# Layer 1's experts in two lots of sequences, with the last sequence's end and the first lot's last sums in gaps of the blocks

## The chip, the cores and the metric

The kernel runs on one core of one Trainium2 chip. The core has five instruction queues that run side by side: TensorE (PE, with its weight loads shown apart as PEld), VectorE (DVE), ScalarE (ACT), GpSimd (POOL) and SyncE (SP). Each runs its own instructions in order, and they wait for one another by semaphores. Transfers between the chip's large memory and the on-chip buffers are issued from SP, ACT and POOL. The metric is the device time of one execution in microseconds (us); the median over several runs is compared.

## The reference

Eight sequences of 512 tokens, 256 wide, in float32, pass through two layers. Each layer is attention, then a mixture of experts, each with the input added and a layer norm after it:

```python
x = _layernorm(x + _L0_attn_ref(x, ...))
x = _layernorm(x + _L0_ffn_ref(x, ...))
x = _layernorm(x + _L1_attn_ref(x, ...))
x = _layernorm(x + _L1_ffn_ref(x, ...))
```

The change concerns the last line. Of twelve experts in layer 1, eight are small networks and four return the token itself. Each token takes its two best:

```python
logits = jnp.einsum('btd,ed->bte', x, gate_w) + expert_bias
topk_logits, topk_idx = jax.lax.top_k(logits, TOP_K)
topk_w = jax.nn.softmax(topk_logits, axis=-1)
...
h = jax.nn.silu(jnp.einsum('btd,efd->btef', x, w1))      # 256 -> 512
y = jnp.einsum('btef,edf->bted', h, w2)                  # 512 -> 256
out = jnp.einsum('bte,bted->btd', w_ffn, y) + w_zero[..., None] * x
```

The kernel computes an expert only for the tokens that chose it.

## The kernel before

Layer 0 and layer 1's attention run in "waves": sixteen waves for each sequence. One wave computes a quarter of the scores of four heads (`scores`), lets ACT make the sigmoids, and multiplies the wave before with the values (`gathered`). The order of all this is written out by hand: `beside1(b, w)` lists for each wave of sequence `b` which small steps of the neighbouring sequences stand beside it. For a sequence `a` those are, in this order: `by_token` and `by_feature` (transposes of the attention's output), `projected` (output projection, router logits and the sums for the norm), `normed3`, `logits`, `chosen` (the two best experts), `counted`, `ranked` (which row of the expert's list a token gets), `sent`, and, two sequences later, `scatter` (L1113), in which POOL writes each token's row, with its gates and its token number, to its place in a table `xbuf1` in the large memory.

Within `with tc.manual_schedule()` the instructions of each engine stand in the order in which the program writes them. Outside it a scheduler orders them.

The last sequence has no later waves to stand beside. So after `waves1(B - 1)` its steps run alone (L1522 to L1528): the last `scatter` of the sequence before, `by_token` to `sent`, its own eight scatters, and `planned` (L1134), which makes from the counts of all eight sequences the table of blocks.

A block is 256 rows of one expert's list. `plan` holds for block `j` its first row and its expert, `mine` a mask of the expert. The program always runs 26 blocks (`NTB0`); two run-time branches (L1636) add more if the counts ask for them. A block `j` has these parts:

- `load(j)` on SP: two register loads from `plan`, one transfer of the block's rows (`xt`), one for each of the expert's two weight matrices. It is called two blocks ahead.
- `turn`: four transposes on PE, a copy on ACT, and on DVE the block's gates `g` and its target rows `to`.
- `inner`: sixteen matmuls, the sigmoid on ACT, the product `h` on DVE.
- `outer`: sixteen matmuls, two scalings on DVE (`yt`), and two scatters on POOL into `ybuf1`, a table with two rows for each token.

In iteration `j` of `work` (L1613) PE's order is `turn(j + 1)`, `inner(j)`, `outer(j - 1)`.

After the blocks and the branches, for each of the eight sequences (L1640): two reads of `ybuf1` on SP, an addition on POOL (L1648) and one on DVE (L1649), the norm's statistics on DVE, a square root on ACT, scale and shift on ACT (L1661), and the output's transfer on ACT's queue (L1665).

Of the kernel before, what the change touches and what calls it, by code (L numbers as in the profile page):

```python
# [9 lines left out]
FP = mybir.dt.float32  # L10
I32 = mybir.dt.int32
# [18 lines left out]
NTB = 2 * NT // TB + E1 - 1  # L30
NTB0, NTB1 = 26, 32
EARLY = 5
NS1 = E1 * NT
# [10 lines left out]
def tile_two_layers(  # L44
# [91 lines left out]
    def row(pool, src, n, name):  # L136
# [5 lines left out]
    slot1 = const.tile([P, NC, E1], FP, name="slot1")  # L142
    nc.gpsimd.iota(
        slot1, pattern=[[0, NC], [NT, E1]], base=-NS1, channel_multiplier=0,
        allow_small_or_imprecise_dtypes=True,
    )

    tok = const.tile([P, B, NC], FP, name="tok")
    nc.gpsimd.iota(
        tok, pattern=[[S, B], [P, NC]], base=0, channel_multiplier=1,  # L150
        allow_small_or_imprecise_dtypes=True,
    )

    full = const.tile([P, E1, NT // TB], FP, name="full")
    nc.gpsimd.iota(
        full, pattern=[[0, E1], [TB, NT // TB]], base=0, channel_multiplier=0,
        allow_small_or_imprecise_dtypes=True,
    )
    block = const.tile([P, NTB], FP, name="block")
    nc.gpsimd.iota(  # L160
        block, pattern=[[1, NTB]], base=0, channel_multiplier=0,
# [12 lines left out]


    xbuf1 = dram.tile([NS1 + TB, XR], FP, name="xbuf1")
    ybuf1 = dram.tile([2 * NT, D], FP, name="ybuf1")
# [174 lines left out]
    def layer0():  # L352
# [64 lines left out]

        def fill(b, part):

            if b == 0:  # L420
                for e in range(2 * part, min(2 * part + 2, E0)):
                    nc.sync.dma_start(
                        out=xbuf[e * CAP : (e + 1) * CAP, :].rearrange("(p c) d -> p c d", p=P),
                        in_=zeros,
                    )
                if part == 3:
                    nc.sync.dma_start(out=ybuf[NSLOT : NSLOT + 1, :], in_=blank[0:1, :D])
                    nc.sync.dma_start(
                        out=xbuf1[NS1 : NS1 + TB, :].rearrange("(c p) d -> p c d", p=P), in_=blanks
                    )  # L430
            for i in range(4 * part, 4 * part + 4):
                at = (b * 16 + i) * 256
                nc.sync.dma_start(
                    out=xbuf1[at : at + 256, :].rearrange("(c p) d -> p c d", p=P), in_=blanks
                )

            if part % 2 == 0:
                at = (b * 2 + part // 2) * 512
                nc.sync.dma_start(
                    out=ybuf1[at : at + 512, :].rearrange("(p c) d -> p c d", p=P), in_=zeros  # L440
                )
# [323 lines left out]
    def layer1(turns):  # L765
# [292 lines left out]
        def counted(b):  # L1058
# [6 lines left out]
            nc.gpsimd.tensor_scalar(q["second"], hot[1][:, :, :E1], float(NT), None, ALU.mult)  # L1065
# [5 lines left out]
        def ranked(b):  # L1071
# [11 lines left out]
            nc.vector.tensor_tensor(q["slot"], pp, slot1, ALU.add)  # L1083
            nc.vector.tensor_copy(counts1[:, 0, :], counts1[:, NC, :])

        def sent(b):
# [10 lines left out]
            nc.vector.tensor_scalar(idx, sf, float(NS1), None, ALU.add)  # L1097
            for k in range(2):
# [9 lines left out]
                tok[:, b].unsqueeze(2).to_broadcast([P, NC, E1]), ALU.add,  # L1108
# [6 lines left out]
        def scatter(b, c):  # L1115
            q = st[b]
            for k in range(2):
                i = nc.gpsimd.indirect_dma_start(  # L1118
                    out=xbuf1[:, :],
# [3 lines left out]
                    bounds_check=NS1 - 1,  # L1123
                    oob_is_err=False,
                )
                apart("xbuf1", i, b == c == k == 0)
# [7 lines left out]
        def planned():  # L1134

            tp = bank()[:, :E1]
            nc.tensor.matmul(out=tp, lhsT=ones, rhs=counts1[:, 0, :], start=True, stop=True)
            more = planp.tile([P, E1, NT // TB], FP, name="more")
            nc.vector.tensor_tensor(more, tp.unsqueeze(2).to_broadcast([P, E1, NT // TB]), full, ALU.is_gt)
            held = planp.tile([P, E1], FP, name="held")  # L1140
            nc.vector.tensor_reduce(held, more, axis=AX.X, op=ALU.add)
            upto = planp.tile([P, E1], FP, name="upto")
            nc.vector.tensor_tensor_scan(upto, ones[:, :E1], held, 0.0, ALU.mult, ALU.add)
            nc.vector.tensor_copy(total, upto[:, E1 - 1 : E1])
            past = planp.tile([P, NTB, E1], FP, name="past")
            nc.vector.tensor_tensor(
                past, upto.unsqueeze(1).to_broadcast([P, NTB, E1]),
                block.unsqueeze(2).to_broadcast([P, NTB, E1]), ALU.is_le,
            )
            which = planp.tile([P, NTB], FP, name="which")  # L1150
            nc.vector.tensor_reduce(which, past, axis=AX.X, op=ALU.add)
            nc.vector.tensor_tensor(past, past, held.unsqueeze(1).to_broadcast([P, NTB, E1]), ALU.mult)
            start = planp.tile([P, NTB], FP, name="start")
            nc.vector.tensor_reduce(start, past, axis=AX.X, op=ALU.add)
            nc.vector.tensor_tensor(start, block, start, ALU.subtract)
            nc.vector.tensor_scalar(start, start, float(TB), None, ALU.mult)
            nc.vector.scalar_tensor_tensor(start, which, float(NT), start, ALU.mult, ALU.add)
            nc.vector.tensor_scalar(plan[:, 0, :], start, float(NS1), None, ALU.min)

            nc.vector.tensor_scalar(which, which, float(E1 - 1), None, ALU.min)  # L1160
            nc.vector.tensor_copy(plan[:, 1, :], which)
            nc.vector.tensor_tensor(
                mine, which.unsqueeze(2).to_broadcast([P, NTB, E1]),
                iota_e[:, 0:1, :E1].to_broadcast([P, NTB, E1]), ALU.is_equal,
            )

# [234 lines left out]
    def beside1(b, w):  # L1401
# [46 lines left out]
        return [[s for s in steps if 0 <= s[1] < B] for steps in plan[w]]  # L1448
# [50 lines left out]
    plan = planp.tile([P, 2, NTB], I32, name="plan")  # L1499
    mine = planp.tile([P, NTB, E1], FP, name="mine")  # L1500
    total = planp.tile([P, 1], I32, name="total")
# [15 lines left out]
    psum(ctx, 2, 2, 2)  # L1517
    with tc.manual_schedule():
# [4 lines left out]
        run([(t.scatter, b - 1, c) for c in range(NC)])  # L1523
        run([(t.by_token, b, c) for c in range(NC)])
        run([(t.by_feature, b, kc) for kc in range(KC)])
        run([(t.projected, b, c) for c in range(NC)])
        run([(fn, b) for fn in (t.normed3, t.logits, t.chosen, t.counted, t.ranked, t.sent)])
        run([(t.scatter, b, c) for c in range(NC)])  # L1528
        t.planned()
    work.close()  # L1530


    with ExitStack() as ph:
        moew = ph.enter_context(tc.tile_pool(name="moew1", bufs=2, side="right"))
        hp = ph.enter_context(tc.tile_pool(name="h1", bufs=3))
        sp = ph.enter_context(tc.tile_pool(name="s1", bufs=4))
        lp = ph.enter_context(tc.tile_pool(name="l1", bufs=3))

        def load(j):
            r = nc.sync.value_load(plan[0:1, 0, j : j + 1], min_val=0, max_val=NS1)  # L1540
            e = nc.sync.value_load(plan[0:1, 1, j : j + 1], min_val=0, max_val=E1 - 1)
            xt = sp.tile([P, TB // P, XR], FP, tag="xt", name="xt")
            nc.sync.dma_start(
                out=xt, in_=xbuf1[bass.ds(r, TB), :].rearrange("(c p) d -> p c d", p=P)
            )
            w = moew.tile([P, 2, KC * F1], FP, tag=("wi", "wo")[j % 2], name="w_e")
            wi = w[:, 0, :].rearrange("p (k f) -> p k f", f=F1)
            nc.sync.dma_start(
                out=wi, in_=w1[bass.ds(e, 1), :, :].rearrange("o (k p) f -> p (o k) f", p=P)
            )  # L1550
            wo = w[:, 1, :].rearrange("p (f d) -> p f d", d=D)
            nc.sync.dma_start(
                out=wo, in_=w2[bass.ds(e, 1), :, :].rearrange("o (f p) d -> p (o f) d", p=P)
            )
            return xt, wi, wo

        def turn(j, xt):

            ps = bank().rearrange("p (k t) -> p k t", t=TB)
            for kc in range(KC):  # L1560
                for c in range(TB // P):
                    nc.tensor.transpose(
                        ps[:, kc, c * P : (c + 1) * P], xt[:, c, kc * P : (kc + 1) * P], ident
                    )
            xtT = hp.tile([P, KC, TB], FP, tag="xtT", name="xtT")
            nc.scalar.copy(xtT, ps)
            gx = sp.tile([P, TB // P, 2, E1], FP, tag="gx", name="gx")
            nc.vector.tensor_tensor(
                gx, xt[:, :, D:XR].rearrange("p c (u e) -> p c u e", e=E1),
                mine[:, j : j + 1, :].unsqueeze(1).to_broadcast([P, TB // P, 2, E1]), ALU.mult,  # L1570
            )
            g = sp.tile([P, TB // P, 2], FP, tag="g", name="g")
            nc.vector.tensor_reduce(g, gx, axis=AX.X, op=ALU.add)
            to = sp.tile([P, TB // P], I32, tag="to", name="to")
            nc.vector.tensor_copy(to, g[:, :, 1])
            return xtT, g, to
# [185 lines left out]
```

## Time and profile before

| | us |
|---|---|
| median of 3 runs | 1662.85 |
| lowest, highest | 1657.31, 1667.59 |
| the profiled execution | 1652.81 |
| its span in the profile | 1651.0 |

| engine | busy us in the span | share |
|---|---|---|
| PE | 1445.3 | 88% |
| DVE | 891.3 | 54% |
| ACT | 677.9 | 41% |
| POOL | 469.1 | 28% |

Layer 0 takes up the span to about 869 us, layer 1's attention the stretch to about 1360, the blocks the stretch from 1400 to 1592, the last sums the rest. Several views are used below. The page divides the span in forty slices. A table of stretches gives, for windows chosen by the reader, each engine's busy time, the TensorE clock that was granted (1.00 is full speed) and the mean share of time in which the 16 DMA engines were busy. The timeline lists groups of instructions by their start, with the idle time of the engine ahead of them and what ended it in brackets. The chain of waits follows the work that ended last back from the end. A busy engine can be one that does more than it must, and idle time is a loss only where the next work had to wait for it.

### The profile page before, as it was taken

To read this page: it belongs to the slowest core of one execution; us is meant where nothing else is said; L and a number is where in the kernel's file an instruction comes from. 1 tells how busy PE (TensorE), PEld (TensorE's weight loads), DVE (VectorE), ACT (ScalarE), POOL (GpSimd) and SP (SyncE) were. 2 spreads that over 40 slices of the span, in tenths; PEclk is the share of its full clock that TensorE was granted. 3 is DMA by queue.
4 is the path that set the end of the run, shared out by engine and by line. 5 is a ranking of instruction groups with operands and counts; after the bars stand their busy time and mean duration, and the time that the engine had idled before them with its cause. 6 is when DMAs were issued, how large, how long until landed. Compare 5 with 4: busy or idle time off the path is not lost. (4 is left out here: it accounts for less than half of the span.)

```text
span 1651.0 us, 24593 instructions
## 1 busy us (share of the span) xinstructions
PE 1445.3 (88%) x8556; PEld 772.2 (47%) x8556; DVE 891.3 (54%) x3367; ACT 677.9 (41%) x1007; POOL 469.1 (28%) x596
## 2 busy tenths in 40 slices
PE   6999889898898789999989999999999993999950
PEld 3444444444444356566534333333333432888840
DVE  3666667666667512220356576677677644333327
ACT  2545445444444320101335666666566660222214
POOL 2221233233232300000251234354453333222233
PEclk8999999999998989999978999999999995999985
DMA  7869920000000102422010000120120003666637
GB/s 221 240 205 362 354 80 12 15 9 20 4 21 1 29 0 79 151 77 89 29 36 8 21 26 25 23 42 26 25 41 18 10 19 114 213 218 216 205 106 238
DMA packets 141385, 149.71 MB, mean 91 GB/s; under 512 B 29006, under 2 KB 126313, under 8 KB 141250
## 3 DMA queue, kind: packets, MB, share of 16 engines
q1 hardware_dynamic: 121954, 120.04, 23.1%
q0 software_dynamic: 10560, 23.51, 5.5%
q10 hardware_dynamic: 8736, 4.46, 0.9%
q8 instruction: 73, 1.20, 0.3%
q14 instruction: 62, 0.51, 0.1%
HBM read 77.01 MB, written 76.83 MB: 93 GB/s over the span
## 5 line engine op out<-in xcount | busy, mean ns | idle before, releaser
L951 ACT ACTIVATE e<-sc 128x1024 f32<-128x1024 f32 x256 | 248.2, 1021 | 146.8 <-PE sc L943 134.5
L514 DVE CUSTOM_DVE_ANT_0 seen<-sc,shade 128x128 f32<-128x128 f32 (+3 forms) x512 | 250.6, 489 | 62.7 <-PE sc L506 33.5
L545 POOL TENSOR_SCALAR_AFFINE_SELECT e<-e 128x256 f32<-128x256 f32 x256 | 103.8, 412 | 630.1 <-ACT e L542 627.4
L542 ACT ACTIVATE e<-sc 128x1024 f32<-128x1024 f32 (+3 forms) x256 | 168.7, 702 | 98.3 <-PE sc L533 90.2
L533 PE MATMUL sc<-q,k 32*128 32x512 f32 (+3 forms) x1024 | 135.7, 501 | 10.9 <-DVE mpad L514 9.9
L506 PE MATMUL sc<-k,q 32*128 32x384 f32 (+3 forms) x1024 | 132.8, 516 | 9.8 <-ACT e L542 5.2
L960 PE MATMUL av<-e,v 128*32 128x512 f32 x1024 | 139.4, 614 | 0.0
L557 PE MATMUL av<-e,v 128*32 128x512 f32 (+3 forms) x1024 | 102.1, 469 | 4.0 <-POOL e L545 3.6
L1337 PE MATMUL sc<-wo,h 128*128 128x256 f32 x448 | 100.5, 381 | 4.8 <-DVE ye L1344 4.8
L1320 PE MATMUL sc<-xeT,wi 128*128 128x512 f32 x224 | 98.1, 593 | 0.9 <-DVE xeT L1306 0.9
L1583 PE MATMUL sc<-xtT,w_e 128*128 128x256 f32 x416 | 95.6, 383 | 0.0
L1603 POOL DMA_INDIRECT ybuf<-yt,to x52 | 50.5, 972 | 156.1 <-DVE yt L1602 122.5
L1597 PE MATMUL yp<-w_e,h 128*128 128x256 f32 x416 | 93.9, 379 | 0.0
L1337 PEld LDWEIGHTS sc<-wo,h 128*128 128x128 f32 x448 | 84.0, 190 | 19.3 <-DVE ye L1344 7.9
L533 PEld LDWEIGHTS sc<-q,k 32*128 32x128 f32 x1024 | 52.3, 190 | 73.3 <-issue 42.6
L943 PE MATMUL sc<-q,kb 32*128 32x512 f32 x512 | 82.0, 640 | 4.8 <-ACT e L951 4.8
L1597 PEld LDWEIGHTS yp<-w_e,h 128*128 128x128 f32 x416 | 79.0, 190 | 10.7
L1583 PEld LDWEIGHTS sc<-xtT,w_e 128*128 128x128 f32 x416 | 78.2, 193 | 9.9
L943 PE MATMUL sc<-q,k 16*128 16x512 f32 x512 | 79.2, 659 | 3.9 <-PEq L1515 2.3
L1589 DVE TENSOR_TENSOR h<-sc,sg 128x1024 f32<-128x1024 f32 x26 | 31.9, 1225 | 93.7 <-ACT sg L1588 90.1
L506 PEld LDWEIGHTS sc<-k,q 32*128 32x128 f32 x1024 | 54.4, 196 | 54.8 <-issue 20.6
L1118 POOL DMA_INDIRECT xbuf<-x,idx x64 | 68.0, 1063 | 26.7 <-issue 15.0
(277 smaller groups left out, 2137.8 us busy)
## 6 DMA issues: line engine op xcount, KB each, us to landing
xbuf<-blank SPq DMA_DIRECT2D x129, 272.0 KB, 6.9
w_e<-in_w SPq DMA_DIRECT2D x52, 512.0 KB, 4.5
ybuf<-blank SPq DMA_DIRECT2D x16, 512.0 KB, 7.0
zt<-ybuf SPq DMA_DIRECT2D x16, 512.0 KB, 5.6
wi<-in_we_in SPq DMA_DIRECT2D x7, 1024.0 KB
wo<-in_we_out SPq DMA_DIRECT2D x7, 1024.0 KB, 9.2
xt<-xbuf SPq DMA_DIRECT2D x26, 272.0 KB, 3.9
own<-in_x SPq DMA_DIRECT2D x8, 512.0 KB, 5.9
```

The costliest lines, as they stand in the source:

```text
L506: nc.tensor.matmul(out=places[r], lhsT=q["q", m, t][32 * r : 32 * r + 32, ib * P : (ib + 1) * P], rhs=q["k", m, t][32 * r : 32 * r + 32, i ...
L514: nc.vector.tensor_tensor_reduce(out=seen[:, :width], in0=places[r], in1=shade[:, :width], scale=-1.0, scalar=-MASKED, op0=ALU.add, op1=AL ...
L533: nc.tensor.matmul(out=places[r], lhsT=q["k", m, t][32 * r : 32 * r + 32, jb * P : (jb + 1) * P], rhs=q["q", m, t][32 * r : 32 * r + 32, : ...
L542: nc.scalar.activation(e[:, :, :width], s[:, :, :width], AF.Exp, scale=SCALE)
L545: nc.gpsimd.affine_select(out=own, in_=own, pattern=[[0, 2], [-1, P]], compare_op=ALU.is_ge, fill=0.0, base=0, channel_multiplier=1,)
L557: nc.tensor.matmul(out=q["av"][32 * r : 32 * r + 32, : (jb + 1) * P], lhsT=vs[b % 2][:, jb, 8 * m + 2 * r + t, :], rhs=es[r], start=(jb == ...
L943: nc.tensor.matmul(out=scs[r // 2][:, r % 2, :], lhsT=k[32 * r : 32 * r + lanes, jb * P : (jb + 1) * P], rhs=q["q", m][32 * r : 32 * r + l ...
L951: nc.scalar.activation(e, scs[pr], AF.Sigmoid, scale=SCALE)
L960: nc.tensor.matmul(out=q["av"][32 * r : 32 * r + 32, :], lhsT=vs[b % 2][:, jb, 8 * m + 2 * r + t, :], rhs=es[r // 2][:, r % 2, :], start=( ...
L1337: nc.tensor.matmul(out=ps[:, c, :], lhsT=h[f][:, c * P : (c + 1) * P], rhs=wo[:, f, :], start=(f == 0), stop=(f == I0 // P - 1),)
L1583: nc.tensor.matmul(out=ps[:, f, :], lhsT=wi[:, kc, f * P : (f + 1) * P], rhs=xtT[:, kc, :], start=(kc == 0), stop=(kc == KC - 1),)
L1597: nc.tensor.matmul(out=ps[:, c, :], lhsT=h[:, f, c * P : (c + 1) * P], rhs=wo[:, f, :], start=(f == 0), stop=(f == F1 // P - 1),)
```

## The change

The eight sequences become two lots, 0 to 4 and 5 to 7. Each lot has tables, counts, plan and mask of its own. Always run are 16 blocks for the first lot and 10 for the second, again 26; one branch at the end runs all further blocks of both lots that could be needed (11 and 9), and the first lot's last sums again.

- In the waves of the last sequence stand the first lot's plan (waves 6, 7, 8), the loads of its first two blocks (10, 12) and the first turn (15).
- The loop over the blocks has four gaps in each iteration: after `turn`, after `inner`, and after each half of `outer`. A list of steps is worked off, one step for each gap. First stand the last sequence's own steps, the scatters of the last two sequences and the second lot's plan (30 steps and so through block 7); from block 17 on stand the last sums of sequences 0 to 4 (30 steps).
- The reads of the last sums bring four consecutive rows to a partition (4 KB in one piece) where they brought one row (1 KB); the token numbers are counted accordingly.
- `outer` is called for each half, so that the first half's scatter is issued before the second half's matmuls. A block's weights come in four transfers, not two, into the buffers of the attention (`half`, `pair`), which stay open.
- The norm's root is made on DVE by three Newton steps (`rsqrt`) where ACT made a square root.
- After the blocks only sequences 5 to 7 are left to be summed.

```diff
-NTB = 2 * NT // TB + E1 - 1
-NTB0, NTB1 = 26, 32
+LOTS = ((5, 16), (3, 10))
...
+    for i, (seqs, always) in enumerate(LOTS):
+        n = seqs * S
+        lot = SimpleNamespace(
+            i=i, first=len(lot_of), n=n, slots=E1 * n, always=always, most=2 * n // TB + E1 - 1
+        )
...
+        lot.xbuf = dram.tile([lot.slots + TB, XR], FP, name=f"xbuf1_{i}")
+        lot.ybuf = dram.tile([2 * n, D], FP, name=f"ybuf1_{i}")
...
             for i in range(4 * part, 4 * part + 4):
-                at = (b * 16 + i) * 256
+                lot, at = placed((b * 16 + i) * 256, E1)
                 nc.sync.dma_start(
-                    out=xbuf1[at : at + 256, :].rearrange("(c p) d -> p c d", p=P), in_=blanks
+                    out=lot.xbuf[at : at + 256, :].rearrange("(c p) d -> p c d", p=P), in_=blanks
                 )
...
+        if b == B - 1:
+            first = lots[0]
+            found[2] += {
+                6: [(t.held, first)],
+                7: [(t.placed, first)],
+                8: [(t.owned, first)],
+                10: [(begun, 0)],
+                12: [(begun, 1)],
+                15: [(turned, 0)],
+            }.get(w, [])
...
+    def load(mem, lot, j):
+        r = nc.sync.value_load(lot.plan[0:1, 0, j : j + 1], min_val=0, max_val=lot.slots)
+        e = nc.sync.value_load(lot.plan[0:1, 1, j : j + 1], min_val=0, max_val=E1 - 1)
+        xt = mem.xt()
+        nc.sync.dma_start(
+            out=xt, in_=lot.xbuf[bass.ds(r, TB), :].rearrange("(c p) d -> p c d", p=P)
+        )
+        w = mem.weights()
+        for k in range(KC):
+            nc.sync.dma_start(
+                out=w[k], in_=w1[bass.ds(e, 1), k * P : (k + 1) * P, :].rearrange("o p f -> p (o f)")
+            )
+        for k in range(2):
+            nc.sync.dma_start(
+                out=w[2 + k].rearrange("p (f d) -> p f d", d=D),
...
+    def last_read(q):
+        lot = lot_of[q.b]
+        for k in range(2):
+            at = k * lot.n + (q.b - lot.first) * S
+            nc.sync.dma_start(
+                out=q.y[k], in_=lot.ybuf[at : at + S, :].rearrange("(p c) d -> p c d", c=NC)
+            )
+
+    def last_sum(q, k):
+        z = q.y[0]
+        (nc.gpsimd, nc.vector)[k].tensor_tensor(z, z, (own[q.b], q.y[1])[k], ALU.add)
...
+    def last_root(q):
+        v = small.tile([P, NC], FP, tag="v3", name="v3")
+        nc.vector.tensor_scalar(v, q.mv[:, :, 1], LN_EPS, None, ALU.add)
+        q.r = rsqrt(v, [P, NC], "r3")
...
+    def last_steps(q):
+        return [
+            (last_sum, q, 0), (last_sum, q, 1), (last_stats, q), (last_root, q), (last_norm, q)
+        ]
+
+    def last(b, pool, bufs):
+        y = pool.tile([P, 2, 2, S], FP, tag="o", name=f"y{b}", bufs=bufs)
...
+        blocks = [(lot, j) for lot in lots for j in range(lot.always)]
+        steps += [(t.by_token, b, c) for c in range(NC)]
+        steps += [(t.scatter, b - 1, c) for c in range(NC)]
+        steps += [(t.by_feature, b, kc) for kc in range(KC)]
+        steps += [None]
+        steps += [(t.projected, b, c) for c in range(NC)]
+        steps += [(fn, b) for fn in (t.normed3, t.logits, t.chosen, t.counted)]
+        steps += [None]
+        steps += [(t.ranked, b), (t.sent, b)]
+        steps += [(t.scatter, b, c) for c in range(NC)]
+        steps += [(t.held, lots[1]), (t.placed, lots[1]), (t.owned, lots[1]), (t.overfull,)]
+        held_back = None
+        for i, (lot, j) in enumerate(blocks):
+            if i + 2 < len(blocks):
+                early.append(load(mem, *blocks[i + 2]))
+            if i == lots[0].always + 1:
+                assert not steps
+                qs = []
+                for b in range(lots[1].first):
+                    qs.append(last(b, att, 2))
+                    steps += [(last_read, qs[b])]
+                    if b > 0:
+                        steps += last_steps(qs[b - 1])
+                steps += last_steps(qs[-1])
+            q = early[i]
+            if i + 1 < len(blocks):
+                turn(early[i + 1])
+                gap()
+            inner(q)
+            gap()
+            if held_back:
+                for c in range(TB // P):
+                    outer(held_back, c)
+                    gap()
+            held_back = q
...
+    more = nc.values_load(over[0:1, 0:1], min_val=0, max_val=lots[0].most)
+    with tc.If(more > 0):
...
+    ends = ctx.enter_context(tc.tile_pool(name="ends", bufs=1))
+    for b in range(lots[1].first, B):
+        q = last(b, ends, B - lots[1].first)
+        last_read(q)
+        run(last_steps(q))
```

## The prediction

> **What bounds the kernel now.** I read the page's forty slices first (PE full in most of them, two holes at the right), then a table of stretches over the last 290 us, then the timeline inside the holes, then the chain of waits. The stretches (columns: window, length, busy us of PE, PEld, DVE, ACT and POOL with instruction counts, granted clock, DMA share, GB/s):
>
> ```profile
> 1340.00:1360.00 20.00, 18.94 (x120) 5.93 (x112) 10.26 (x62) 12.90 (x16) 4.29 (x5) 1.00 0.03 10
> 1360.00:1380.00 20.00, 9.09 (x34) 6.67 (x34) 15.15 (x80) 0.89 (x3) 8.09 (x9) 0.72 0.08 27
> 1380.00:1400.00 20.00, 1.98 (x9) 1.64 (x10) 5.28 (x22) 2.29 (x5) 7.84 (x8) 0.50 0.46 155
> ...
> 1540.00:1560.00 20.00, 20.00 (x100) 17.64 (x99) 6.98 (x15) 4.38 (x6) 4.23 (x5) 1.00 0.69 220
> ...
> 1600.00:1620.00 20.00, 0.00 (x0) 0.00 (x0) 12.38 (x29) 2.97 (x7) 13.47 (x5) 0.50 0.98 301
> ```
>
> Attention and the expert blocks are PE bound. Between them PE is nearly idle for 40 us, and after the blocks it has no work for 60 us. The timeline gives the edges (start, us, engine, line):
>
> ```profile
> 1354.32 2.88 PE L960 MATMUL av<-e,v 128*32 128x512 f32 x16
> ...
> 1389.06 0.97 POOL L1118 DMA_INDIRECT xbuf<-x,idx  x1 [0.31 <-issue]
> 1391.76 0.41 SPq L1543 DMA_DIRECT2D xt<-xbuf  x1
> ...
> 1399.98 5.09 PE L1583 MATMUL sc<-xtT,w_e 128*128 128x256 f32 x16
> ```
>
> Attention ends at 1357.2 and the first block's matmuls start at 1399.98: the 42.8 us are one chain (the last sequence's projection, norm, router, eight scatters, the plan, then the first load).
>
> ```profile
> 1584.66 7.07 PE L1597 MATMUL yp<-w_e,h 128*128 128x256 f32 x32
> ...
> 1591.77 0.88 DVE L1602 TENSOR_SCALAR yt<-yp,g 128x256 f32<-128x256 f32 x2 [2.58 <-PE yp L1597]
> 1592.53 0.97 POOL L1603 DMA_INDIRECT ybuf<-yt,to  x1 [1.20 <-DVE yt L1602]
> 1595.68 0.97 POOL L1603 DMA_INDIRECT ybuf<-yt,to  x1 [2.18 <-issue]
> 1599.67 27.46 SPq L1644 DMA_DIRECT2D zt<-ybuf  x16
> 1604.70 2.34 POOL L1648 TENSOR_TENSOR own<-own,zt 128x1024 f32<-128x1024 f32 x1 [8.05 <-DMA zt<-ybuf]
> ```
>
> PE ends at 1591.73, the first read of ybuf leaves at 1599.67 (7.9 later), and the span ends at 1651.0 (51.3 later). Blocks come every 7.345 us (their scatters stand at 1567.48 and 1574.82); 26 of them take 191.75.
>
> [...] 0.50 in the hole, and the first block's 16 matmuls take 5.09 us against 3.62 later. [...] the tiny L1659 takes 1.45 us while POOL adds, 0.15 once POOL is done. [...] DMA share 0.98 at 301 GB/s.
>
> **Part 1, the first hole.** Plan, loads and first turn of lot 0 stand in the last sequence's waves; its end stands in the gaps of blocks 0 to 7. What was latency becomes PE work: 16 transposes L976 (2.6 us), 8 of L997 (1.7), 8 matmuls L1009 (3.2 in the chain of waits), 4 of L1074/L1077 (1.3 at low clock). That is 8.8 at most; I take 8. The first lot's plan and first turn add 0.9 to the waves, the second turn 0.6. The blocks lose the cold start (5.09 - 3.62 = 1.5): 190.2. I allow 1.5 for edges, such as the copy of the last av (0.59) that the first transposes wait for. PE end: 1357.2 + 0.9 + 0.6 + 8 + 190.2 + 1.5 = 1558.4, **33.3 earlier** (25 to 36). The DVE steps (some 18 us between 1358 and 1380) hide beside blocks, where DVE is busy 7 us in 20; the densest iteration holds norm, logits and choice (about 10.6 us with its block) and lags 3 us, against 4.65 us from the end of h (1565.55) to the outer matmul that reads it (1570.2). The POOL scatters hide too. SP issues 5 transfers a block for 3: 5 x 0.56 + 1.2 for the two register loads = 4.0 of 7.35, hidden. Two xbufs keep lot 0's loads from waiting for later scatters; filling them costs one more DMA at the start, beside attention.
>
> **Part 2, the number of blocks.** 26 stay, but only if 16 and 10 suffice. Routing the reference's inputs gives 474, 463, 429, 551, 464, 492, 248, 278 rows for sequences 0 to 4 (2+2+2+3+2+2+1+2 = 16 blocks of 256) and 224, 280, 225, 375, 250, 224, 250, 176 after (10): exactly full, the nearest edge 6 rows away. These are the kernel's inputs: 5,403 rows of 1 KB are 5.53 MB, and the blocks' software queue moved
>
> ```profile
> q0 software_dynamic: 2496, 5.54, 7.0%
> ```
>
> **Part 3, the first lot's last sums.** Five sequences add per sequence 1.05 MB of reads and 0.52 written, 2.34 us POOL, about 7 DVE (sum 1.23, statistics 1.75, root and less 2.6, waits), 2.07 ACT; no PE. DVE and ACT have room; the order does not. A third read reuses the first's buffer, so on SP it waits for sequence 0's output, and **queued behind it on SP are the loads of block 21 on**. The stall, with t from PE's start of iteration 17: lot 0's last scatter starts at 0.8 (1591.77, 1592.53) and lands 2.4 to 4 later (4.0 at the end of the old run): reads 0 and 1 leave at 4. The first half lands at 9.0 (1599.67 to 1604.70 is 5.0); POOL to 11.4, DVE sum 12.6; then, in DVE's order, the block's gate sums 0.5, statistics, h 1.2, root: 18.7; ACT to 20.9; output 0.4 + 3.3 (its median to landing) = 24.5. Read 2 leaves then; block 21's xt follows 2.2 later behind 1 MB and lands at about 31. PE wants it at 3 x 7.35 = 22.0: **9 us**. Read 3, the same way, leaves at 38 and block 23's xt lands at 44.5, wanted at 45.7: nothing. Read 4 leaves at 53.8, block 24's xt lands at 60, wanted at 53: **7**. Sum **16**, bounds 0 (xt slips by, or the chain is shorter) and 32 (DMA: 7.9 MB more over 66 us is 120 GB/s on top of 220, more than the 301 seen at full share). ACT's and POOL's waits inside these steps also hold sigmoids and scatters; they lie inside the same stalls.
>
> **Part 4, the end.** The last scatter no longer follows its pair, since each half is sent as it is done: 0.8 + 4.0 after PE, about 5 instead of 7.9: **3 less** (0 to 3.5). Then three sequences, not eight. DVE's order puts the third sum before the first "less", so: fifth half landed 11.0 after the first read (1610.7 before), POOL 2.8, third sum 1.2, some 8 small operations 2.0, then about 19 (3.8) and 11 (2.4) for the other two, ACT 2.1, output 0.4 + 4.7: 30.4 instead of 51.3, **20.9 less** (17 to 25). The root on DVE costs 13 operations of 0.16 each, counted here, and removes the 1.28 us table load, which nothing waited for.
>
> **Sum.** Against the profiled execution, 1652.81 (span 1651.0 and 1.8 around it): -33.3 + 16 - 3 - 20.9 = -41.2, so 1611.6. The median of the runs shown, 1662.85, is 0.6% above that execution; from it the forecast is **1621.6**.
>
> **Rivals.**
> A (62%): the forecast.
> B, the reads cost PE nothing (18%): 1605.6. For it: the waves' trace shows SP idle, and xt issues about two blocks ahead. Against: the order on SP above.
> C, contention doubles the stalls or the DVE lag reaches PE (14%): 1637.6, up to 1655 with both. For it: 340 GB/s asked. [...]
> D, the other side (4%): a lot overflows, and the run-time branch executes all 20 further blocks and five more sums. Even at 7.35 each that is 147 more: at least 1768. It decides from one row too many, that is 6 tokens that route differently; the 5.54 MB speak against it.
> E, the change does not overlap (2%): the steps serialise with the blocks as before and only the order changes: 1650 to 1665.
>
> **Numbers.** A measurement of this kernel can tell about 1% from no change. Faster by over 1% means under 1646: A, B and most of C. Within 1%: E, and a part of C. Slower: D and a sliver of unseen waits. Range 1601 to 1642: B's fast side and C's middle, each with the bounds of parts 1 and 4.
>
> **What would show it.** Right: the hole at 1360 to 1400 is gone, PE at clock 1.0 through it; 26 scatter pairs; PE waits for xt at blocks 21 and 24, some 9 and 7 us, with SP behind a read of ybuf; about 30 us from first final read to end. Wrong: PE gaps at other blocks, a block cadence above 7.35 in lot 0 beyond 8 us in sum, no stall at 21, or any work of the branch.

## The result and the profile after

| | us |
|---|---|
| after, median of 12 runs | 1670.59 (1667.55 to 1681.47) |
| before, median of 12 runs beside them | 1660.72 (1653.06 to 1670.83) |
| ratio after to before | 1.0061, 95% interval 1.0033 to 1.0089 |
| the profiled execution of after | 1680.0, its span 1678.2 |

The kernel became slower by 0.6%, where 2.5% faster was forecast. Attention does not end at the same time in two executions: at 1357.2 us in the profile of before, at 1374.6 in that of after, and between 1345 and 1372 in those of the experiments. So the profiles are compared here from the end of attention to the end of the span. That stretch took 293.8 us before (1651.0 - 1357.2) and 303.6 after (1678.2 - 1374.6): 9.8 more, as much as the medians differ (9.9). The whole loss lies there.

The first thing to look at is the hole that the change was to fill. In the table of stretches of the kernel after (columns as in the prediction's first excerpt):

```profile
1360.00:1380.00 20.00, 19.96 (x126) 9.36 (x124) 8.47 (x52) 12.91 (x18) 0.29 (x1) 1.00 0.76 235
1380.00:1400.00 20.00, 17.18 (x89) 14.74 (x90) 9.49 (x25) 3.70 (x6) 9.35 (x10) 1.00 0.54 169
...
1480.00:1500.00 20.00, 17.92 (x86) 15.14 (x85) 5.11 (x12) 3.22 (x4) 4.57 (x5) 1.00 0.58 175
...
1640.00:1660.00 20.00, 0.74 (x4) 0.31 (x2) 4.95 (x7) 0.00 (x0) 7.83 (x4) 0.57 0.44 170
```

The hole is gone: PE is full up to the end of attention and goes on at clock 1.00. But in the blocks it is busy 17.2 and 17.9 us of 20, where before it was full, and it still has work at 1640. From the first block's matmul (1375.47) to PE's end (1640.74) are 265.3 us, against 191.75 for the bare blocks before and some 216 in the forecast (190.2 + 8 + 16 + 1.5). The costliest groups on the page (busy and mean ns of one, then idle time ahead and what ended it) name the line. Before:

```profile
L1597 PE MATMUL yp<-w_e,h 128*128 128x256 f32 x416 | 93.9, 379 | 0.0
```

and after:

```profile
L1677 PE MATMUL yp<-w_e,h 128*128 128x256 f32 x416 | 108.8, 408 | 50.0 <-DVE yt L1682 48.3
```

The same 416 matmuls of `outer` had no idle time ahead of them; now they have 50 us, of which 48.3 wait for DVE's `yt`. The timeline of one iteration in the middle of the first lot (`inner` of block 10, `outer` of block 9), with no steps in its gaps, shows how (kernel after; start, us, engine, line, in brackets the idle time ahead):

```profile
1482.61 1.89 PE L1677 MATMUL yp<-w_e,h 128*128 128x256 f32 x8
1482.81 1.02 ACT L1666 ACTIVATE sg<-sc 128x1024 f32<-128x1024 f32 x1 [2.87 <-PE sc L1660]
1483.87 1.23 DVE L1668 TENSOR_TENSOR h<-sc,sg 128x1024 f32<-128x1024 f32 x1 [3.94 <-ACT sg L1666]
...
1485.01 0.47 DVE L1682 TENSOR_SCALAR yt<-yp,g 128x256 f32<-128x256 f32 x1
...
1485.54 1.99 PE L1677 MATMUL yp<-w_e,h 128*128 128x256 f32 x8 [1.04 <-DVE yt L1682]
...
1494.19 1.59 PEld L1677 LDWEIGHTS yp<-w_e,h 128*128 128x128 f32 x8 [1.44 <-DVE yt L1682]
```

`outer` is called once for each half. The first half's eight matmuls start at 1482.61; the second half's wait until DVE has read the first half out of `yp`: both halves lie in one PSUM tile, `yp`, of 512 numbers of 4 bytes in a partition. And DVE is not free to read it: in its order `h` of the newer block stands ahead of `yt`, and `h` waits for the sigmoid, which waits for the end of `inner`. So sigmoid (1.02), `h` (1.23) and `yt` (0.47) stand between the two halves, beside only 1.89 us of matmuls. PE idles 1.04 us in each block without steps, and these blocks come every 8.65 us (1485.54 to 1494.19) instead of every 7.345.

What demands the wait between DVE's reading and the next matmuls no run shows. What they show is where it goes: PE waits 48.3 us in all for `yt` in this kernel, and 1.3 us when each half has a tile of its own and nothing else is changed (first experiment).

The end of the kernel after, from the timeline:

```profile
1638.21 0.48 DVE L1682 TENSOR_SCALAR yt<-yp,g 128x256 f32<-128x256 f32 x1 [1.24 <-PE yp L1677]
1638.75 1.99 PE L1677 MATMUL yp<-w_e,h 128*128 128x256 f32 x8 [0.58 <-DVE yt L1682]
1640.78 0.48 DVE L1682 TENSOR_SCALAR yt<-yp,g 128x256 f32<-128x256 f32 x1 [2.09 <-PE yp L1677]
1643.02 0.97 POOL L1683 DMA_INDIRECT ybuf<-yt,to  x1 [3.07 <-issue]
1648.35 3.06 SPq L1700 DMA_DIRECT2D y<-ybuf  x6
```

The first two lines are the last block's. No `inner` follows it, so neither sigmoid nor `h` stands ahead of `yt`, and DVE was idle when the first half ended; PE still waits 0.58 us, the length of `yt` (0.48) and 0.1 around it. So of the 1.04 us in the other blocks 0.58 come with the common tile alone, and 0.46 from what stands ahead of `yt` on DVE.

The last scatter starts 1.8 us after its `yt` is done, with no wait that the profile shows, and the first final read follows 5.3 after that: 7.6 us after PE's end, against 7.9 before. From this read to the end of the span are 29.9 us; before 51.3.

### The profile page after: what moved, and what is told of

It reads as the page before. It is cut to its first block, busy times and chain, and to the rows that moved or that the text cites. A ratio compares the mean times of both kernels' runs of the same rounds, so it can differ in the third digit from the quotient of the medians.

```text
span 1678.2 us, 24883 instructions
## 1 busy us (share of the span) xinstructions
PE 1470.0 (88%) x8558; PEld 778.2 (46%) x8558; DVE 905.1 (54%) x3481; ACT 674.3 (40%) x998; POOL 472.8 (28%) x598
## 5 line engine op out<-in xcount | busy, mean ns | idle before, releaser
L1677 PE MATMUL yp<-w_e,h 128*128 128x256 f32 x416 | 108.8, 408 | 50.0 <-DVE yt L1682 48.3
L976 PE MATMUL av<-e,v 128*32 128x512 f32 x1024 | 143.8, 634 | 0.0
L959 PE MATMUL sc<-q,k 16*128 16x512 f32 x512 | 84.3, 668 | 6.7 <-ACT e L967 3.2
L522 PEld LDWEIGHTS sc<-k,q 32*128 32x128 f32 x1024 | 54.3, 196 | 54.7 <-issue 20.9
L506 ACT ACTIVATE q<-mm,bq_t,lanes 128x256 f32<-128x256 f32 x60 | 30.6, 560 | 104.4 <-PE mm L499 104.4
```

Of the source, the lines that this page charges most:

```text
L522: nc.tensor.matmul(out=places[r], lhsT=q["q", m, t][32 * r : 32 * r + 32, ib * P : (ib + 1) * P], rhs=q["k", m, t][32 * r : 32 * r + 32, i ...
L959: nc.tensor.matmul(out=scs[r // 2][:, r % 2, :], lhsT=k[32 * r : 32 * r + lanes, jb * P : (jb + 1) * P], rhs=q["q", m][32 * r : 32 * r + l ...
L976: nc.tensor.matmul(out=q["av"][32 * r : 32 * r + 32, :], lhsT=vs[b % 2][:, jb, 8 * m + 2 * r + t, :], rhs=es[r // 2][:, r % 2, :], start=( ...
L1677: nc.tensor.matmul(out=q.ps[:, c, :], lhsT=q.h[:, f // 2, at : at + P], rhs=q.wo[f // 2][:, f % 2 * D : (f % 2 + 1) * D], start=(f == 0), ...
```

## The experiments

Theory: the split of `outer` within one tile costs what the parts of the change bring. First rival: the steps in the gaps load DVE so much that it is late for everything, with or without a common tile. Second rival: the first lot's reads or the other traffic in the blocks cost it. All times of one table row come from one chip; between chips the kernel before itself took 1642.7 to 1665.2, so ratios are compared. A median of a changed kernel is over two to six runs.

| kernel | median | before beside it | ratio, 95% interval |
|---|---|---|---|
| two tiles | 1628.42 | 1665.22 | 0.9781 (0.9730 to 0.9831) |
| both halves first | 1623.30 | 1665.22 | 0.9748 (0.9704 to 0.9791) |
| before, split | 1690.87 | 1665.22 | 1.0145 (1.0094 to 1.0196) |
| two tiles, sums late | 1651.91 | 1665.22 | 0.9899 (0.9850 to 0.9948) |
| one tile, sums late | 1687.03 | 1652.47 | 1.0197 (1.0139 to 1.0256) |
| third buffer | 1613.74 | 1652.47 | 0.9744 (0.9709 to 0.9779) |
| end in written order | 1613.94 | 1652.47 | 0.9762 (0.9727 to 0.9797) |
| both halves first, again | 1602.45 | 1642.70 | 0.9763 (0.9748 to 0.9778) |
| third buffer, again | 1597.33 | 1642.70 | 0.9724 (0.9711 to 0.9737) |
| later norm | 1593.81 | 1642.70 | 0.9699 (0.9680 to 0.9717) |

### Two tiles

The kernel after, with a PSUM tile of its own for each half; order and call by halves stay.

```diff
-            q.ps = p["av"].tile([P, S], FP, tag="av", name="yp").rearrange("p (c d) -> p c d", d=D)
             q.yt = q.mem.yt()
+        ps = p["av"].tile([P, S], FP, tag="av", name="yp")[:, :D]
```

> The changed kernel, but each half of outer gets a PSUM tile of its own. Theory P (PE waits for DVE because both halves share one tile; 48.3 us of PE waits on yt in the changed kernel's profile): the waits on yt go, blocks come every 7.35 us again, and the time falls by 34 to 48 us from 1670.6, to 1622-1637. Theory D (DVE is overloaded by the steps in the gaps, and the shared tile only shows where PE notices it): PE waits for h instead, the time stays above 1655. Theory S (the SP queue stalls block 21 and 24, as forecast, and was hidden by the slower blocks): P's fall comes less 16 us, with waits on xt, about 1640-1650.

Measured: ratio 0.9781, and PE needs 222.4 us from the first block's matmul to its end instead of 265.3. Nothing else was changed, so the common tile costs the kernel after some 43 us, net of what PE now waits for elsewhere. The waits of PE in the blocks of this kernel (total, times, longest):

```profile
PE mm L1641 <- DMA xt<-xbuf: 13.8, 2, 7.2
...
PE yp L1677 <- DVE yt L1682: 1.3, 1, 1.3
```

The wait for `yt` is gone but for one of 1.3 us, and there stand the two stalls that the prediction had named, at the turns of blocks 21 and 24, with 6.6 and 7.2 us. In the kernel after they are not to be seen: there SP's reads wait for outputs too (32.1 us in three waits), and the slower blocks leave the loads that much more time. The time lies where theory P put it, though the stalls of theory S are there, which put it at 1640 to 1650. The first rival falls: DVE does the same work in the same order, and PE does not wait for it.

### Both halves first

The kernel after with one tile as it is, but both halves' matmuls ahead of both scalings and scatters, as in the kernel before.

```diff
     def outer(q, c):
+        products(q, c)
+        if c == TB // P - 1:
+            for c in range(TB // P):
+                scaled(q, c)
```

> The changed kernel, but the two halves' matmuls first and then both scalings and scatters, as in the kernel before; the tile stays shared, the gap after the first half stays. Theory P: as fast as with two tiles within 5 us (1622-1640), since no matmul follows a reading of its own tile. Theory D: above 1655. If the early first scatter is worth something, this one is slower than two tiles by up to 3 us.

Measured: ratio 0.9748 and later, on a second chip, 0.9763. The blocks took 216.5 us. So the tile may stay; it is enough that nothing of DVE stands between the halves. It is no worse than two tiles (0.9781, the intervals overlap): sending the first half's scatter early is not seen to bring anything in the total (in the profile the first final read follows PE's end by 7.1 us with two tiles and by 8.1 here). PE's remaining waits are above all 11.5 us for `xt` in two stalls. The timeline of this kernel shows the first (the last two lines are from the timeline of PE alone):

```profile
1517.26 0.41 ACTq L1736 DMA_DIRECT2D out<-y  x1
...
1520.41 0.82 SPq L1708 DMA_DIRECT2D y<-ybuf  x2
...
1522.59 0.39 SPq L1619 DMA_DIRECT2D xt<-xbuf  x1
...
1526.05 1.09 PE L1641 MATMUL mm<-ident,xt 128*128 128x128 f32 x4 [6.41 <-DMA xt<-xbuf]
1526.93 5.06 PE L1660 MATMUL sc<-xtT,w_e 128*128 128x256 f32 x16
1531.83 3.62 PE L1682 MATMUL yp<-w_e,h 128*128 128x256 f32 x16
```

A sequence's output leaves at 1517.26; the read into its buffer goes 3.15 later, when the output has landed; the block's rows, queued behind on SP, go at 1522.59, 2.2 after that, and PE turns them at 1526.05. This is the chain of the prediction's Part 3 (output 0.4 + 3.3, then `xt` 2.2 later).

A stall costs more than its wait. The turn behind it takes 1.09 us where others take 0.60, and the next sixteen matmuls 5.06 where the following take 3.62. The table of stretches shows the granted clock fall from 1.00 to 0.66:

```profile
1510.00:1520.00 10.00, 9.64 (x47) 8.15 (x45) 6.63 (x27) 3.59 (x6) 4.86 (x4) 1.00 0.53 189
1520.00:1530.00 10.00, 3.95 (x12) 3.39 (x13) 9.45 (x26) 0.59 (x1) 4.81 (x4) 0.66 0.87 297
```

From the first matmul of block 9 to PE's end this kernel takes 144.0 us, the kernel before 127.6. The 16.3 more are the 11.5 of waits and 4.8 that show as no wait.

### The kernel before, with the split alone

The kernel before, with each half's scaling and scatter directly behind its matmuls; nothing else of the change.

```diff
                         start=(f == 0), stop=(f == F1 // P - 1),
                     )
-            for c in range(TB // P):
                 nc.vector.tensor_scalar(yt[:, c, :], ps[:, c, :], g[:, c, 0:1], None, ALU.mult)
```

> The kernel before, with one edit: each half's scaling and scatter directly behind its matmuls, so that the second half's matmuls follow the reading of the first half in the same tile. Theory P: every block is 1.3 us longer (7.35 to 8.65), 26 blocks: +34 us, 1695. Theory D: no steps stand in gaps here, so no change beyond 5 us.

Measured: ratio 1.0145; from the first block's matmul to PE's end 225.0 us against 191.75: 33.3 more (33.5 from the end of attention to the span's end), which is 1.28 us for each of 26 blocks; the cadences differ by 1.30 (8.65 - 7.345). PE's waits in its blocks:

```profile
PE yp L1597 <- DVE yt L1601: 26.5, 26, 1.0
```

Every block waits, 25 of them by 1.04 us and the last, as in the kernel after, by 0.58. The rest of the 1.30 shows as longer matmuls: the two runs of eight take 1.89 and 1.99 us, 0.26 more than one run of sixteen (3.62). What makes them longer no run separates, and the ends of matmuls are modelled in the profile. The split alone turns the kernel before into a slower one. It needs no step in a gap, no read and no second lot, so the second rival falls too as the main cause.

### The sums late, with two tiles and with one

Two kernels in which all eight sequences' last sums stand behind the blocks, so that the blocks' gaps hold only the last sequence's steps: one with two tiles, one with the common tile of the kernel after.

```diff
-                for b in range(lots[1].first):
-                    qs.append(last(b, att, 2))
-                    steps += [(last_read, qs[b])]
...
-    for b in range(lots[1].first, B):
+    for b in range(B):
         q = last(b, ends, B - lots[1].first)
```

With two tiles:

> Two tiles, and the last sums of all eight sequences after the blocks, none in gaps. It gives up part 3 and 4 of the forecast and keeps part 1 (33 us). Theory P: 1660.7 - 33 = 1628, within 6. Theory S: the difference to two tiles with the sums in the gaps is then only some 5 us (20.9 + 3 gained at the end, 16 lost to stalls, counted from here); without S it is 20 or more (this one slower).

With the common tile:

> The changed kernel as it is (shared tile, scaling after each half), but all last sums after the blocks. It differs from the version with two tiles and late sums (1651.9; 204.5 us from the first block's matmul to PE's end) by the shared tile alone. Theory P: 34 us of waits for the cadence and up to 14 more where the last sequence's steps on DVE hold the scaling: 239 to 252 us from the first matmul to PE's end, 1686-1700. Theory D: less than 10 us more.

Measured, from the first block's matmul to PE's end:

| | last sequence's steps only | with the first lot's sums |
|---|---|---|
| a tile for each half | 204.5 | 222.4 |
| common tile | 245.0 | 265.3 |

The common tile costs 40.5 us without the sums and some 43 with them. 33.3 of it is the bare block (the split of before); the rest lies in the blocks whose gaps hold steps, where waits of up to 7.1 us show steps standing ahead of `yt` on DVE. The wait of PE with the sums late, in the kernel with the common tile:

```profile
PE yp L1677 <- DVE yt L1682: 33.5, 24, 7.1
```

The sums in the gaps cost PE 18.0 with two tiles and 20.3 with one. With two tiles and no sums in the gaps PE ends 205.3 us after attention; before it was 234.5. So the first hole's filling brought 29.2 us in this kernel.

The total of 1651.91 with two tiles misses the 1628 that was expected, for a reason at the end: from the first final read to the span's end are 71.8 us, not the 51.3 of before. The eight sequences share three buffers there, and a read waits for the output that leaves from the same buffer; in the waits of SP's queue that is 46 us in five waits. It is a cost of that kernel's buffers, and its blocks alone are used here.

### A third buffer for the first lot's sums

Both halves first, and a third buffer, so that the third sequence's read waits for no output.

```diff
-                    qs.append(last(b, att, 2))
+                    qs.append(last(b, lotp, 1) if b == 2 else last(b, att, 2))
```

> The version with both halves' matmuls first (1623.3; PE waits 11.5 us for xt in two places), with a third buffer for the reads of the last sums, so that the third, fourth and fifth read no longer wait for the output just issued. Theory S (a read that waits for an output holds the loads queued behind it on SP): both waits on xt go, 1612 (1609-1615). Rival C (the loads are late because the DMA engines are full in these blocks): waits on xt of 6 us or more stay, 1618 or above.

> The kernel with both halves' matmuls ahead of both scalings and a third buffer, again, for a comparison on one chip: a ratio to the kernel before near 0.974, PE waiting for h some 8 us and not for xt.

> The kernel with both halves' matmuls ahead of both scalings, with two buffers, again, on the chip of the version with three: a ratio to the kernel before near 0.975 and PE waiting for xt some 11 us. If the third buffer only exchanges one wait for another, as the two ratios 0.9748 and 0.9744 on two chips say, the two differ by less than 3 us; if chips hid a gain, this one is 5 us or more slower.

Measured: 0.9744 at first, on another chip than the kernel with two buffers (0.9748), as if nothing came of it. On one chip, 0.9724 against 0.9763: 5.1 us between the medians, with intervals that do not touch. So the waits for `xt` were the order on SP, as theory S had it: no such wait is left. But the gain is less than the 11.5 us of waits that went, since PE now waits for `h` (7.2 us in the second run); the blocks took 212.1 us instead of 216.3. The timeline of its first run shows what is late next:

```profile
1549.93 0.97 POOL L1691 DMA_INDIRECT ybuf<-yt,to  x1 [0.30 <-issue]
1550.26 3.06 DVE L241 SCALAR_TENSOR_TENSOR r<-r3a,r 128x4 f32<-128x4 f32 x1
1550.91 2.37 POOL L1714 TENSOR_TENSOR y<-y,own 128x1024 f32<-128x1024 f32 x1
...
1554.14 2.07 ACT L1733 ACTIVATE y<-y,less,r 128x256 f32<-128x256 f32 x4 [7.92 <-DVE less L1728]
...
1556.67 1.02 ACT L1666 ACTIVATE sg<-sc 128x1024 f32<-128x1024 f32 x1 [0.46 <-PE sc L1660]
...
1557.72 1.22 DVE L1668 TENSOR_TENSOR h<-sc,sg 128x1024 f32<-128x1024 f32 x1 [3.09 <-ACT sg L1666]
...
1559.00 2.21 PE L1682 MATMUL yp<-w_e,h 128*128 128x256 f32 x9 [2.60 <-DVE h L1668]
```

ACT had waited 7.9 us for DVE's root with its norm, and a block's sigmoid stood behind it; then `h` was late, and PE waited. A part of the root's lateness is the operation at 1550.26: 128x4 numbers, which take 0.16 us in other places, took 3.06. It started in POOL's scatter (1549.93 to 1550.90), ahead of the start that the profile gives for POOL's addition (1550.91), and ended as the addition did (1553.3). The end of the kernel before shows the like: its 128x4 operation L1659 takes 1.45 to 1.60 us beside POOL's additions, and 0.15 or 0.16 after the last of them; here such a delay stands in the blocks. What joins the two no run shows, since none was made without POOL's addition there.

### The end in the order of the program

The kernel with the third buffer, with the last three sequences' sums in the order in which they are written: three reads, then the steps of one sequence after the other, instead of the scheduler's order.

```diff
+    with tc.manual_schedule():
+        qs = [last(b, ends, B - lots[1].first) for b in range(lots[1].first, B)]
+        for q in qs:
+            last_read(q)
+        for q in qs:
+            run(last_steps(q))
```

> The same, and the last three sequences' sums in an order written by hand (all of one sequence, then the next) instead of the scheduler's, which puts the third sum before the first root. If DVE's order sets the end: 1 to 4 us less than without. If reads, POOL's additions and the last output set it: the same within 1.

Measured: from the first final read to the span's end 33.3 us instead of 29.4; the ratio, 0.9762, cannot be told from the 0.9744 beside it. Neither expectation came true, 1 to 4 us less or the same within 1: the scheduler's order is the better one, by 3.9 us in one profiled execution of each.

### The norm one step later

The kernel with the third buffer, with each sequence's norm behind the next sequence's first sum.

```diff
-                        steps += last_steps(qs[b - 1])
-                steps += last_steps(qs[-1])
+                        now = last_steps(qs[b - 1])
+                        steps += now[:1] + norm + now[1:4]
+                        norm = now[4:]
+                    else:
+                        norm = []
+                now = last_steps(qs[-1])
+                steps += now[:1] + norm + now[1:]
```

> The kernel with both halves' matmuls ahead of both scalings and a third buffer for the first lot's sums, with one thing moved: each sequence's norm on ACT stands one step later, behind the next sequence's first sum, so that ACT does not stand before a block's sigmoid and wait for DVE's root (in the version with three buffers ACT waited 38.4 us for that in the last 85 us of blocks, and PE 8.7 us for h). Theory, that this order is what holds h: PE's waits for h (8.7) fall under 3, the blocks from their first matmul to PE's end take about 208 instead of 215.2, and the kernel is 5 to 8 us faster than the version with three buffers, at a ratio to the kernel before of about 0.971. Rival, that DVE's own share (sum and statistics ahead of h) holds it: ACT's wait for the root shrinks, PE's wait for h stays at 7 or more, the time within 2 us of three buffers. Second rival: outputs come later, so a read into a buffer that is used again waits longer on SP and holds xt, 5 us or more of PE waiting for xt.

Measured: ratio 0.9699, in the medians 3.5 us less than three buffers on the same chip (the intervals just overlap, at 0.9711 to 0.9717). In the profiled executions the blocks took 205.6 us instead of 212.1. The waits in the last stretch of the kernel with the third buffer (second run), of ACT and of PE:

```profile
ACT y L1733 <- DVE less L1728: 37.9, 5, 9.3
...
PE yp L1682 <- DVE h L1668: 7.2, 2, 4.0
```

and with the later norm:

```profile
ACT y L1733 <- DVE less L1728: 21.7, 5, 6.3
...
PE yp L1682 <- DVE h L1668: 3.7, 3, 1.7
...
PE mm L1641 <- DMA xt<-xbuf: 0.5, 1, 0.5
```

PE's wait for `h` fell by 3.5, the blocks by 6.5. Again waits cost more than their length. The granted clock in the stretch from 1500 to 1520 was 0.86 with the third buffer and 1.00 with the later norm. These matmuls stand behind the longest wait for `h` of each kernel:

```profile
1516.21 6.22 PE L1682 MATMUL yp<-w_e,h 128*128 128x256 f32 x16 [4.03 <-DVE h L1668]
1539.03 3.72 PE L1682 MATMUL yp<-w_e,h 128*128 128x256 f32 x16 [1.72 <-DVE h L1668]
```

The sixteen matmuls behind the wait of 4.03 us took 6.22 us, those behind 1.72 us hardly more than the usual 3.62. The blocks came out as expected (about 208). The medians fell by less than the 5 to 8 us, and the wait did not fall under 3: ACT still waits 21.7 us for the root, so the order could be drawn apart further. Neither rival holds: the wait for `h` is not 7 or more, and outputs did not come late enough to hold `xt` (0.5). This version is the fastest of all, by 3% against before.

## Why the prediction was wrong

The forecast was 41.2 us less than before; measured from the end of attention it was 9.8 more. The 51 us between them lie so. The first three measured rows are the steps from before to two tiles with the sums late, from there to one tile with the sums late, and from there to after, so they add up by construction:

| term, us against before | forecast | measured |
|---|---|---|
| Part 1, the first hole | -33.3 | -29.2 (two tiles, sums late) |
| the split of `outer` within one tile | none | +40.5 |
| Part 3, the first lot's sums | +16 | +20.3 (18.0 with two tiles) |
| Part 4, start of the final reads | -3 | -0.3 |
| Part 4, three sequences instead of eight | -20.9 | -21.4 |
| sum | -41.2 | +9.9 |

**The step that failed** is the first sentence of Part 4. It took the call of `outer` by halves for a gain only, an earlier last scatter worth 3 us, and left the other side unpriced: that DVE's reading of the first half now stands between two runs of PE matmuls in every block. The prediction followed the new reads to the loads that stand behind them on SP; it did not follow the moved scaling to the matmuls that now wait for it. The material was at hand. Before, a block's 16 matmuls of `outer` ran without a wait and `yt` came after them; the diff puts `yt` between; and the timeline of before gives `h` 1.23 and the sigmoid 1.02, both ahead of `yt` in the new order, where a half has only 1.89 us of matmuls to cover them. Part 1 did weigh DVE's lag, but against the 4.65 us from the end of `h` to its reader, the slack of the old order; for the new reader, the second half, there was none. In its place the runs show a wait of 1.04 us in each bare block, 1.30 of cadence, 33.3 us in 26 blocks (the kernel before with the split alone), and 40.5 with the steps in the gaps. One of the prediction's own signs of being wrong, a block cadence above 7.35 in lot 0, came true.

**Part 1** held by its mechanism: PE runs through the end of attention at clock 1.00, and 29.2 of 33.3 us came with two tiles. In the kernel with both halves first, the stretch from the end of attention to the first matmul of block 9, which holds the steps, is 32.6 us shorter than before (74.3 against 106.9). The 0.9 us that the prediction put into the waves lie ahead of the end of attention and are not seen here. Its premise that the steps in the gaps hide on DVE fails above all through the common tile; there they lengthen the waits (40.5 against 33.3 for bare blocks).

**Part 2** held: the blocks' matmuls are 416 as before, and nothing of the branch ran.

**Part 3** held in its mechanism, but only where blocks come at their old pace: waits of 6.6 and 7.2 us at blocks 21 and 24, with SP behind a read that waits for an output, where 9 and 7 were worked out. Its size came out in part by luck. With both halves first the waits are only 11.5 us, and 4.8 us of slower matmuls behind them, which the prediction counts at the cold start and not here, bring the sum to 16.3. In the kernel after the slower blocks cover the stalls, and the sums cost PE about as much by their DVE work ahead of `yt`. So the mark "no stall at 21" came about for another reason than the prediction meant.

**Part 4's other half** held (-21.4 for -20.9). The 3 us for the start of the final reads did not come: the last scatter started 2.3 after PE's end instead of 0.8, and the first read 5.3 after it instead of 4.0. The prediction took the last scatter to follow its pair, but its own excerpt has 2.18 us of idle POOL ahead of that scatter, with no wait shown. Such a gap (3.07) stands there in the kernel after as well; its cause stays open. Even with two tiles the first final read stands 7.1 us after PE's end (before: 7.9).

**The rivals.** None had the mechanism. C came nearest, with "the DVE lag reaches PE", but priced it from the DVE work of the steps, not from a wait in each block, and 1637.6 was far off. E came nearest in number (1650 to 1665), but looked for the loss in an overlap that fails, and the overlap works. The rival for the slower side, D, was a mishap of counts, and no run shows it; the "sliver of unseen waits" beside it had no place and no price. What was missing was a rival on the slower side that asks of every edit what now waits for what, small edits too; 1.30 us in 26 blocks is 34 us.

The forecast without this one step fits the kernel that has the rest of the change. Both halves first, against before: 32.6 us less to the first matmul of block 9 (forecast 33.3), 16.3 more from there to PE's end (16), the first final read 0.2 later, and 22.1 less from it on (20.9). That is 38.3 less, where the forecast without the 3 us of the early scatter is 38.2.

## What to carry to other kernels

When an edit cuts a run of matmuls in two and puts a reader of the first part between them, look at whether both parts write the same PSUM tile, and at what stands ahead of that reader on its engine: here the matmuls then paid, in each turn of the loop, at least the reader's own time (0.48 us, a wait of 0.58) and more where the chain ahead of the reader outlasted the first part (1.04). Either keep all matmuls ahead of all readers or give each part a tile of its own; the two came out alike here (0.9748 and 0.9781 of before). A small delay within a loop body should be multiplied by the loop's count before it is called small, and behind a wait that is removed (`xt`, then `h`) the next in the same order is to be looked for before its length is booked as gain. A wait of PE is to be priced with the matmuls behind it: behind one of 4.03 us here, sixteen took 6.22 us instead of 3.62, in a stretch with a granted clock of 0.86.

## What was not expected of the hardware

- The end of attention, which none of the edits touches but for a few small steps, moved by up to 29 us between executions (1345.1 to 1374.6) on different chips and kernels. Medians of the kernel before differed by 1.4% between chips (1642.70 to 1665.22). A change of 1% is to be read from its own stage or from runs on one chip.
- A wait of PE cost more than its length. Waits of 1.04 us cost 1.30 each; two waits of 11.5 us in all cost 16.3; and behind one of 4.03 us sixteen matmuls took 6.22 us instead of 3.62.
- A 128x4 operation on DVE took 3.06 us, against 0.16 elsewhere, beside POOL's scatter and addition of 128x1024 numbers, in the midst of blocks and not only at the end.
